# Sums of exponentials folded on VectorE instead of TensorE, and channel sums broadcast by way of DRAM

## The chip, the cores and the metric

The kernel runs on one core of a Trainium2 chip. The metric is the device time of one execution in microseconds (us), given as the median over runs. Lower is better. The core has TensorE (PE, with its weight loads listed apart as PEld), VectorE (DVE), ScalarE (ACT), GpSimd (POOL) and SyncE (SP, here only an issuer of DMAs). [...]

## What is computed

Two layers of a graph network on 16 graphs of 1024 nodes with 256 channels, all in float32. The parts that the change touches lie in the first layer:

```python
h = relu(layernorm(x))                                  # per graph: 1024 nodes x 256 channels
c = mean(h, axis=channels)                              # one number per node
A = abs(abs(sigmoid(c[None, :] - c[:, None]) - 0.5) - 0.5) * 2
Wg = adj * (A + A.T) * 0.5                              # 1024 x 1024
q = relu((h.T @ Wg) * para).T ; k, v = split(h @ kv_w)  # 4 heads of 64
attn = softmax(q @ k.T * scale)                         # over the 1024 keys
x = x + attn @ v
```

The second layer normalises again, multiplies by a normalised adjacency matrix and passes two linear maps with batch norms over all graphs and nodes. The kernel computes A from tanh(|difference| / 2), with the sums of h over the channels in place of the means.

## The kernel before

**Units and steps.** A graph's attention is cut into four units (L871): two channel chunks k (two heads each) by two halves f of 512 queries. A unit has four steps, and each step takes two blocks of 128 keys. `scores` (L851) multiplies a key block with 512 queries for both heads (keys on partitions, two heads by 512 queries in the free dimension) and ScalarE takes the exponential (L867). `Unit.add` (L880) adds the 8 tiles `p` of a unit up into `acc` on VectorE (L886, L889): what is left to sum for the softmax's denominators are the 128 partitions of `acc`. `Unit.values` (L891) multiplies p with the values, one step late, into `o`.

**The end of a unit.** When the last values are issued (step 0 of the next unit), `Unit.sums` (L911) multiplies `acc` with a 128x64 matrix of ones, once for each head; ScalarE copies the result to `row` (L919, a tile of the four-buffer tag "y"), and POOL's queue stores one row a head to DRAM and reads it back with the queries on partitions (L920, L925). Two steps later (three in graph 0), `Unit.finish` (L929) transposes the output `o` by head and query on TensorE into `ot`, and `add_output` (L940) takes the reciprocal (L943), scales (L944) and adds to x (L950). The sums' tile and `ot` share one PSUM buffer, tag "t".

**The order of the work** is written out by hand in `attention` (L957), which goes through 256 steps, 16 a graph, and emits for each: the step's scores; what is due at the top (finish, a background piece that asked for the top by yielding TOP); add_output; the two adds; the values of the step before; then background pieces. `background(b)` (L761) is a generator that yields the cost of each piece, mostly 1.71 for eight matmul instructions; the loop takes pieces until the graph's total times the elapsed share of its 16 steps is reached (L1002), and a TOP ends the step early. For a middle graph b the background is: keys of graph b+1 (4 pieces), its `queries` (14), its values (4), `aggregate` (L622) of graph b-1 (14 pieces, called the gather), then `prepare(b+2)` (L743), which weaves in `hidden(b-1)` (8). Between them go VectorE's and ScalarE's parts: `weigh` (L395), which makes the weights from the channel sums by Abs (L426), Tanh (L434) and a product with adj (L413), the second norm of graph b-1 (in queries) and the first norm of graph b+2 (in the gather, from piece 7). `take` (L488), the q sums (L496 to L522), `at` (L649 to L675, scaled at L646) and the batch statistics (L717) take TensorE's results off PSUM or prepare its operands. `soon` (L116) defers an action to the next piece.

**Channel sums.** `Norm` (L286) finds mean and variance on VectorE (L305, L307), the inverse square root on POOL (L82, L83), the shift on VectorE (L315 for the second norm, L318), and ScalarE's relu (L329) leaves the channel sums of a node block in `csum`, 128 partitions by 8 blocks. The Abs needs all 1024 sums in the free dimension of every partition: `columns_of` (L184) repeats each column over 128 elements (L189, tiles of tag "y"), `broadcast_row` (L195) transposes the eight blocks on TensorE (L200), and ScalarE copies them to `cbc` (L201).

**Graph 0's extra work.** `graph` (L231) combines blocks of the transposed adjacency on POOL and stores them to `aht_d` from tiles `two` and `one`, of tag "y" too; `degrees` (L212) sums the columns of adj.

```python
# the loop's body, in its order
made = scores(*unit.at, g)
...
    ended.finish()
if top:
    done += advance(bg)
...
    ended.add_output()
...
    unit.add(pr)
...
    last.values(g_last, prs)
    if g_last == NG - 1:
        last.sums()
...
while done < due and not top:
    cost = advance(bg)
```

## Time and profile before

| what | us |
|---|---|
| median of 3 runs (2646.86 to 2647.53) | 2647.13 |
| the profiled execution, whole | 2651.18 |
| its span, first to last instruction | 2649.3 |
| PE busy | 2571.1 |
| DVE busy | 1741.8 |
| ACT busy | 1335.5 |
| POOL busy | 561.2 |
| sums' matmuls (L917), busy | 65.8 |
| broadcasts' transposes (L200), busy | 18.1 |
| POOL issuing the sums' DMAs (L920, L925) | 37.5 + 98.2 |

Busy time is the union over an engine's instructions[...]. An instruction's idle time is what its engine waited just before it, with what ended the wait. A float32 matmul shows as two instructions, a transpose as one. The granted TensorE clock was 0.989 of full speed over the span.

### The profile page before, as it was taken

What the parts mean: (1) busy time and instruction counts of PE and PEld (TensorE: products, weight loads), DVE (VectorE), ACT (ScalarE), POOL (GpSimd) and SP (SyncE); (2) the same over time, 40 slices, a digit from 0 to 9 for tenths busy, and PEclk for the clock granted to TensorE, in tenths of its full rate; (3) what the DMA queues carried; (4) which work ended last, traced back from release to release, by engine and by line L of the source; (5) the groups of instructions that cost most, each with busy time, mean ns of one, the idle gap of its engine ahead of it and who ended that gap; (6) DMA issues with size and microseconds to landing.
All of it is one profiled execution on the core that took longest, in us unless ns stands there. A gap on an engine that the chain in (4) does not pass through costs nothing. (4 is left out here: it accounts for less than half of the span.)

```text
span 2649.3 us, 32166 instructions
## 1 busy us (share of the span) xinstructions
PE 2571.1 (97%) x11874; PEld 951.7 (36%) x11874; DVE 1741.8 (66%) x2766; ACT 1335.5 (50%) x1935; POOL 561.2 (21%) x648
## 2 busy tenths in 40 slices
PE   8979999999999999999999999999999999999994
PEld 3333333333333333333333333333333333334443
DVE  5648576766667675757666676757576675557675
ACT  5745454636364554546363645545463634335544
POOL 1451111021111111110211111111111112026653
PEclk9989999999999999999999999999999999999997
DMA  4453414242423323152525242332424232355559
GB/s 159 149 177 109 146 61 171 84 171 80 166 78 135 100 96 136 60 175 80 172 80 175 68 144 92 103 133 65 166 80 171 80 132 96 134 196 204 193 179 377
DMA packets 132870, 356.12 MB, mean 134 GB/s; under 512 B 19040, under 2 KB 35936, under 8 KB 126560
## 3 DMA queue, kind: packets, MB, share of 16 engines
q1 hardware_dynamic: 105952, 274.77, 29.7%
q0 software_dynamic: 26752, 79.20, 8.9%
q8 instruction: 96, 1.57, 0.2%
q14 instruction: 70, 0.57, 0.1%
HBM read 279.19 MB, written 74.72 MB: 134 GB/s over the span
## 5 line engine op out<-in xcount | busy, mean ns | idle before, releaser
L867 ACT ACTIVATE p<-sc 128x1024 f32<-128x1024 f32 x512 | 495.4, 1020 | 610.3 <-PE sc L859 609.8
L889 DVE TENSOR_TENSOR acc<-acc,p 128x1024 f32<-128x1024 f32 x384 | 470.9, 1226 | 135.5 <-ACT p L867 115.1
L859 PE MATMUL sc<-q,k 64*128 64x512 f32 x2048 | 510.2, 617 | 14.2 <-ACT p L867 14.2
L900 PE MATMUL o<-p,v 128*64 128x512 f32 x2048 | 497.6, 607 | 0.0
L159 PE MATMUL pg<-w,h_a 128*64 128x512 f32 x1600 | 358.1, 592 | 3.4 <-ACT k L600 1.7
L159 PE MATMUL pa<-aht,h_b 128*64 128x512 f32 x1536 | 343.7, 592 | 0.0
L859 PEld LDWEIGHTS sc<-q,k 64*128 64x128 f32 x2048 | 176.6, 186 | 335.0 <-issue 298.0
L920 POOL DMA_DIRECT2D sums_d<-row x64 | 37.5, 586 | 1031.8 <-ACT row L919 1031.8
L159 PE MATMUL py<-at,w 128*64 128x512 f32 x1024 | 230.4, 592 | 0.0
L900 PEld LDWEIGHTS o<-p,v 128*64 128x64 f32 x2048 | 124.6, 136 | 286.0 <-issue 284.5
L413 DVE SCALAR_TENSOR_TENSOR w<-w,adj 128x1024 f32<-128x1024 f32 x128 | 158.0, 1235 | 101.7 <-ACT w L434 97.8
L159 PEld LDWEIGHTS pg<-w,h_a 128*64 128x64 f32 x1600 | 115.5, 137 | 231.8 <-issue 213.1
L159 PEld LDWEIGHTS pa<-aht,h_b 128*64 128x64 f32 x1536 | 111.2, 137 | 212.6 <-issue 196.6
L713 ACT ACTIVATE y<-py,vec 128x512 f32<-128x512 f32 x128 | 87.6, 684 | 167.9 <-PE py L159 111.4
L426 ACT ACTIVATE w<-cbc,csum 128x512 f32<-128x512 f32 x256 | 170.0, 715 | 0.0
L886 DVE TENSOR_TENSOR acc<-p,p 128x1024 f32<-128x1024 f32 x64 | 78.9, 1233 | 109.3 <-ACT p L867 109.3
L714 POOL DMA_DIRECT2D y_d<-y x128 | 70.1, 547 | 316.1 <-ACT y L713 315.5
L434 ACT ACTIVATE w<-w 128x1024 f32<-128x1024 f32 x128 | 134.9, 1054 | 1.8
L488 DVE TENSOR_TENSOR w<-w,w 128x1024 f32<-128x1024 f32 x112 | 132.7, 1215 | 1.5
L925 POOL DMA_DIRECT2D inv<-sums_d x128 | 98.2, 771 | 138.7 <-DMA sums_d<-row 102.2
L159 PEld LDWEIGHTS py<-at,w 128*64 128x64 f32 x1024 | 74.3, 137 | 145.1 <-issue 128.2
L717 DVE BATCH_NORM_STATS2 stats<-y 128x6 f32<-128x512 f32 x128 | 85.4, 686 | 59.3 <-ACT y L713 57.4
(151 smaller groups left out, 2892.9 us busy)
## 6 DMA issues: line engine op xcount, KB each, us to landing
aht<-aht_d SPq DMA_DIRECT2D x224, 512.0 KB, 6.4
adj<-in_adj_dram SPq DMA_DIRECT2D x128, 512.0 KB, 4.4
y_d<-y POOLq DMA_DIRECT2D x128, 256.0 KB, 2.6
yin_f<-y_d SPq DMA_DIRECT2D x32, 1024.0 KB, 6.3
x<-in_x_dram SPq DMA_DIRECT2D x32, 512.0 KB, 5.0
para<-in_para_dram SPq DMA_DIRECT2D x64, 256.0 KB, 3.8
x_d<-x POOLq DMA_DIRECT2D x16, 1024.0 KB, 10.5
xo_f<-x_d SPq DMA_DIRECT2D x32, 512.0 KB, 8.7
```

The source lines that it names most:

```text
L159: nc.tensor.matmul(dst[r], left[:, r], right, start=start, stop=stop)
L413: nc.vector.scalar_tensor_tensor(w, w, 1.0, a, op0=ALU.add, op1=ALU.mult)
L426: nc.scalar.activation(w[:, t, :], cbc[:, q * FB : (q + 1) * FB], AF.Abs, bias=csum[:, th * TH + t : th * TH + t + 1], scale=-1.0,)
L434: nc.scalar.activation(made[i], made[i], AF.Tanh, scale=-0.5 / C)
L488: nc.vector.tensor_sub(block(i)[part], block(x)[part], block(y)[part])
L713: nc.scalar.activation(y, made, AF.Identity, bias=b1[:, j : j + 1])
L717: nc.vector.bn_stats(stats1[:, j, i, :], y)
L859: nc.tensor.matmul(sc[:, e, :], ks[b][k][r, m * P : (m + 1) * P], qs[b][k][r, f * FB : (f + 1) * FB], start=True, stop=True,)
L867: nc.scalar.activation(pr, sc, AF.Exp)
L889: nc.vector.tensor_add(self.acc, self.acc, pr)
L900: nc.tensor.matmul(self.o[r, :], vs[b][k][:, m, r], pr[:, e, :], start=(m == 0), stop=(m == NT - 1),)
L925: nc.gpsimd.dma_start(out=self.inv[:, :, e], in_=sums_d[u][e].rearrange("(j q) -> q j", q=P))
```

## The change

Two edits, each with its followers.

**Sums of exponentials.** `fold` turns one head's half of `acc` (128 x 512) in squares of 32 x 32 on VectorE into PSUM and reduces each square's rows: 128 x 16 partial sums `part`, in which partition 32a + r holds, for query c*32 + r, the sum over 32 of the partitions. The four groups of partitions are added by one matmul with `same`, a 128 x 128 matrix that is one where two indices are equal modulo 32; so each group of 32 partitions holds all sums, and four reciprocals, each on 32 partitions, take those that the partition needs. The first head is folded at the end of step 0, the second at the end of step 1, the matmul stands at the top of step 2 and the transposes of the output at the top of step 3, one step later than before (the last unit's folds both stand at the end of its step 0, the rest at the next top).

**Channel sums.** For graphs 1 to 15 `csum` is written to DRAM as it lies (32 contiguous bytes a partition) and read back by one DMA to all partitions, both on SP's queue. `cbc` then holds node t*128 + p at p*8 + t, and the Abs reads it with a step of 8 elements. Graph 0 keeps the way by TensorE. `prepare` loses a TOP piece of cost 1.0 for each graph, and so does the start of the background of graph 0. The norm and the sums' way by DRAM go into the gather from piece 3. `st6` and `mv` have one buffer instead of two.

```diff
@@ -69,13 +69,22 @@
     aht_d = dram.tile([7, NP // 2, P, TH, FB], F32, name="aht_d")
     y1_d = [dram.tile([P, HC, FB], F32, name=f"y1_d{i}") for i in range(B * NH)]
+    csum_d = [dram.tile([N], F32, name=f"csum_d{b}") for b in range(B)]
     dinv_d = dram.tile([N], F32, name="dinv_d")
-    sums_d = [dram.tile([2, FB], F32, name=f"sums_d{u}") for u in range(B * CC * NH)]
     UNITS = B * CC * NH
     seen = const.tile([P, 2, UNITS], F32, name="seen")
-    ones = const.tile([P, HD], F32, name="ones")
+    ones = const.tile([P, 1], F32, name="ones")
     nc.gpsimd.memset(ones, 1.0)
+
+    SQ = 32
+    NS = P // SQ
+    same = const.tile([P, NS, SQ], F32, name="same")
+    nc.vector.tensor_reduce(
+        same[:, 0, :], ident.rearrange("p (a r) -> p r a", r=SQ), AX.X, ALU.add
+    )
+    for i in range(1, NS):
+        nc.vector.tensor_copy(same[:, i, :], same[:, 0, :])
     def rsqrt(dst, src, add, tmp):
@@ -290,8 +299,8 @@
             def __init__(self, b, first):
                 tag = "a" if first else "b"
                 self.src = xs[b]
-                self.st6 = p2.tile([P, NT, 6], F32, tag="st6", name=f"st6_{tag}_{b}")
-                self.mv = p2.tile([P, NT, 2], F32, tag="mv", name=f"mv_{tag}_{b}")
+                self.st6 = p1.tile([P, NT, 6], F32, tag="st6", name=f"st6_{tag}_{b}")
+                self.mv = p1.tile([P, NT, 2], F32, tag="mv", name=f"mv_{tag}_{b}")
                 self.sm = p2.tile([P, 3, NT], F32, tag="lnsm", name=f"lnsm_{tag}_{b}")
                 self.csum = None
                 if first:
@@ -386,11 +395,23 @@
                     )
                 nc.vector.tensor_copy(ht[:, g * FB : (g + 1) * FB], pt)
-        def differences(b, cbs):
-
-            cbcs[b] = p1.tile([P, N], F32, tag="cbc", name=f"cbc_{b}")
-            broadcast_row(cbcs[b], cbs, f"c{b}")
+        def differences(b):
+
+
+            cbc = p1.tile([P, N], F32, tag="cbc", name=f"cbc_{b}")
+            cbcs[b] = (
+                cbc.rearrange("p (t q) -> p t q", t=NT)
+                if b == 0
+                else cbc.rearrange("p (q t) -> p t q", t=NT)
+            )
             weighers[b] = weigh(b)
+            if b == 0:
+                broadcast_row(cbc, columns_of(csums[b], f"c{b}"), f"c{b}")
+                return
+            nc.sync.dma_start(out=csum_d[b].rearrange("(p t) -> p t", p=P), in_=csums[b])
+            nc.sync.dma_start(
+                out=cbc, in_=csum_d[b].rearrange("(o n) -> o n", o=1).to_broadcast([P, N])
+            )
         def weigh(b):
@@ -424,8 +445,8 @@
                     made.append(w)
                     for t in range(TH):
                         nc.scalar.activation(
-                            w[:, t, :],
-                            cbc[:, q * FB : (q + 1) * FB],
+                            w[:, t, :].rearrange("p (t q) -> p t q", q=P),
+                            cbc[:, q * NT // NH : (q + 1) * NT // NH],
                             AF.Abs,
                             bias=csum[:, th * TH + t : th * TH + t + 1],
                             scale=-1.0,
@@ -740,14 +761,15 @@
                 yield from norm.half(half * NT // 2)
             nc.gpsimd.dma_start(out=x1_d[B - 1], in_=xs[B - 1])
+        def summed(b):
+            yield from Norm(b, True).all()
+            differences(b)
+            yield 0.0
+
         def prepare(b, products):
-            cbs = columns_of(csums[b], f"c{b}")
             yield from islice(products, 1)
-            yield TOP
-            differences(b, cbs)
-            yield 1.0
             w = weighers[b]
             for k in range(CC):
                 yield from weave(islice(products, 3), (0, islice(w, AHEAD // 2)))
@@ -761,10 +783,7 @@
         def background(b):
             if b == 0:
-                differences_1 = columns_of(csums[1], "c1")
-                yield TOP
-                differences(1, differences_1)
-                yield 1.0
+                differences(1)
                 for k in range(CC):
                     yield TOP
                     transposed(1, k)
@@ -776,6 +795,7 @@
                 yield from weave(
                     plain_queries(1), (0, norm), (0, w), (5, graph()), (7, degrees())
                 )
+                differences(2)
                 yield from islice(products, 2)
                 yield from prepare(2, products)
                 return
@@ -793,7 +813,7 @@
                 yield from weave(endings.pop(), (2, normed(b - 1)))
                 yield next(gather)
             if b + 2 < B:
-                yield from weave(gather, (7, Norm(b + 2, True).all()))
+                yield from weave(gather, (3, summed(b + 2)))
                 yield from prepare(b + 2, before)
             elif b + 2 == B:
@@ -908,22 +928,33 @@
                     self.os = p2.tile([P, FB], F32, tag="os", name=f"os_{self.name}")
                     nc.scalar.copy(self.os, self.o)
+            def fold(self, e):
+
+
+                if e == 0:
+                    self.part = p1.tile([P, 2, FB // SQ], F32, tag="part", name=f"part_{self.name}")
+                pt = ps_t.tile([P, FB], F32, tag="t", name=f"turned_{self.name}_{e}")
+                nc.vector.transpose(pt, self.acc[:, e, :])
+                nc.vector.tensor_reduce(
+                    self.part[:, e, :], pt.rearrange("p (c s) -> p c s", s=SQ), AX.X, ALU.add
+                )
+
             def sums(self):
-                u = self.index
-                pt = ps_t.tile([P, FB], F32, tag="t", name=f"sums_{self.name}")
-                for e in range(2):
-                    r = slice(e * HD, (e + 1) * HD)
-                    nc.tensor.matmul(pt[r, :], ones, self.acc[:, e, :], start=True, stop=True)
-                row = py.tile([P, FB], F32, tag="y", name=f"row_{self.name}")
-                nc.scalar.copy(row, pt)
-                nc.gpsimd.dma_start(
-                    out=sums_d[u], in_=row.rearrange("(e r) c -> e r c", r=HD)[:, 0, :]
+                pt = ps_t.tile([P, FB], F32, tag="t", name=f"sums_{self.name}")[:, : 2 * FB // SQ]
+                nc.tensor.matmul(
+                    pt,
+                    same.rearrange("p a r -> p (a r)"),
+                    self.part.rearrange("p e c -> p (e c)"),
+                    start=True,
+                    stop=True,
                 )
                 self.inv = p2.tile([P, FB // P, 2], F32, tag="inv", name=f"inv_{self.name}")
-                for e in range(2):
-                    nc.gpsimd.dma_start(
-                        out=self.inv[:, :, e], in_=sums_d[u][e].rearrange("(j q) -> q j", q=P)
+                for a in range(NS):
+                    r = slice(a * SQ, (a + 1) * SQ)
+                    nc.vector.reciprocal(
+                        self.inv[r].rearrange("p j e -> p e j"),
+                        pt[r].rearrange("p (e j a) -> p a e j", e=2, a=NS)[:, a],
                     )
             def finish(self):
@@ -940,7 +971,6 @@
             def add_output(self):
                 b, k, f = self.at
                 J, pt = FB // P, self.out
-                nc.vector.reciprocal(self.inv, self.inv)
                 nc.vector.tensor_mul(
                     self.os.rearrange("p (j e c) -> p j e c", j=J, e=2),
                     pt.rearrange("p (j e c) -> p j e c", j=J, e=2),
@@ -960,7 +990,7 @@
             steps = [(u, g) for u in units for g in range(NG)]
             per_graph = CC * NH * NG
             before = None
-            pending = []
+            at_top, at_end, adds = {}, {}, {}
             bg, done, total, top = iter(()), 0.0, 0.0, False
             for s in range(len(steps) + 2):
                 if s < len(steps):
@@ -978,15 +1008,13 @@
                     due = total * (s % per_graph + 1) / per_graph
                 else:
                     due += 5.1
-                ended = None
-                if pending and pending[0][1] <= s:
-                    ended = pending.pop(0)[0]
-                    ended.finish()
+                for action in at_top.pop(s, ()):
+                    action()
                 if top:
                     done += advance(bg)
                     top = False
-                if ended is not None:
-                    ended.add_output()
+                if s in adds:
+                    adds.pop(s)()
                 if s < len(steps):
                     for pr in made:
                         unit.add(pr)
@@ -994,11 +1022,13 @@
                     (last, g_last), prs = before
                     last.values(g_last, prs)
                     if g_last == NG - 1:
-                        last.sums()
-
-
-                        later_by = 3 if last.at[0] == 0 else 2
-                        pending.append((last, s + (later_by if last.index < UNITS - 2 else 1)))
+
+                        n = 0 if last.index == UNITS - 1 else 1
+                        for e in range(2):
+                            at_end.setdefault(s + n * e, []).append(lambda u=last, e=e: u.fold(e))
+                        at_top.setdefault(s + 1 + n, []).append(last.sums)
+                        at_top.setdefault(s + 1 + 2 * n, []).append(last.finish)
+                        adds[s + 1 + 2 * n] = last.add_output
                 while done < due and not top:
                     cost = advance(bg)
                     if cost is None:
@@ -1007,6 +1037,8 @@
                         top = True
                         break
                     done += cost
+                for action in at_end.pop(s, ()):
+                    action()
                 before = (steps[s], made) if s < len(steps) else None
             run(bg)
...
@@ -1051,7 +1083,7 @@
                 run(islice(products, 2))
                 for k in range(CC):
                     transposed(0, k, (1,))
-                differences(0, columns_of(csums[0], "c0"))
+                differences(0)
                 run(weave(products, (0, islice(weighers[0], AHEAD))))
                 load_x(1)
                 load_x(2)
...
```

More of the change, by code (lines that the diff above doesn't have):

```diff
@@ L1018, in layers @@
                     run(Norm(b, True).all())
-                    differences(b, columns_of(csums[b], f"c{b}"))
+                    differences(b)
                     for k in range(CC):
@@ L1339, in flag @@
     def flag(good):
-        nc.tensor.matmul(good[0:1, :], ext[:, 2:3], ones[:, 0:1], start=True, stop=True)
+        nc.tensor.matmul(good[0:1, :], ext[:, 2:3], ones, start=True, stop=True)
         nc.vector.tensor_scalar(bad, good[0:1, :], -1.0, float(P), op0=ALU.mult, op1=ALU.add)
```

## The prediction

> **What bounds the kernel now.** I read the page's first two parts, then the stretches, then the timeline of one graph. In part 1 the columns are busy time, share of the span and instructions; part 2 cuts the span into 40 slices.
>
> ```profile
> PE 2571.1 (97%) x11874; PEld 951.7 (36%) x11874; DVE 1741.8 (66%) x2766; ACT 1335.5 (50%) x1935; POOL 561.2 (21%) x648
> PE   8979999999999999999999999999999999999994
> ```
>
> TensorE is never free for long, so its queue sets the time. The stretches say where it isn't full. The first line is graph 6, the second graph 0 (stretch; length, PE, PEld, DVE, ACT and POOL busy; clock, DMA):
>
> ```profile
> 923.10:1068.30 145.20, 145.01 (x698) 51.91 (x696) 98.24 (x156) 74.11 (x109) 22.42 (x29) 1.00 0.34 117
> 61.80:196.90 135.10, 115.81 (x548) 42.81 (x546) 72.34 (x111) 78.62 (x116) 70.58 (x95) 0.92 0.48 160
> ```
>
> Graphs 1 to 13 start 145.2 us apart, each with PE covered throughout. Graph 0 has 19.3 us (135.1 - 115.8) without a matmul. The timeline there names the cause (start, length, instruction, idle time before it and its releaser):
>
> ```profile
> 174.97 0.59 ACT L919 COPY row<-sums 128x512 f32<-128x512 f32 x1 [19.63 <-DMA aht_d<-two]
> ...
> 176.54 3.40 PE L859 MATMUL sc<-q,k 64*128 64x512 f32 x8 [13.73 <-ACT p L867]
> ...
> 183.41 1.12 PE L200 MATMUL cbp_c<-ident,cb_c 128*128 128x128 f32 x4 [2.88 <-DVE v L617]
> ```
>
> `row` and the columns `cb` share the four "y" buffers with graph()'s `two` and `one`, whose stores hold them. ScalarE waits, the exponentials queue behind it, and TensorE stops.
>
> In the steady graphs the sums are plain PE work: a step where they run is 9.8 us long and its neighbour 8.9. In the lines below the sums' weights load at 926.79, and the next work's at 927.65: **0.86 us a unit**. The broadcast's eight transposes hold PE from 1043.39 to 1044.41: **1.02 us a graph**.
>
> ```profile
> 926.79 0.14 PEld L917 LDWEIGHTS sums<-acc,ones 128*64 128x64 f32 x2 [0.28 <-issue]
> 927.65 0.14 PEld L159 LDWEIGHTS pk<-ht,kvw_f 128*64 128x64 f32 x2 [0.29 <-issue]
> 1043.39 1.09 PE L200 MATMUL cbp_c<-ident,cb_c 128*128 128x128 f32 x8
> 1044.41 1.94 PE L900 MATMUL o<-p,v 128*64 128x512 f32 x8
> ```
>
> What decides is how far VectorE is behind at the top of a unit's third step (the next unit's step 2), since the new sums will stand there. Today the output transposes `ot` stand there on PE, and `inv` (L943) marks the same place on VectorE:
>
> ```profile
> 942.56 1.22 DVE L413 SCALAR_TENSOR_TENSOR w<-w,adj 128x1024 f32<-128x1024 f32 x1
> 943.69 0.20 DVE L943 RECIPROCAL inv<-inv 128x8 f32<-128x8 f32 x1
> 943.75 0.66 PE L935 MATMUL ot<-ident,os 128*128 128x128 f32 x4
> ...
> 980.93 0.66 PE L935 MATMUL ot<-ident,os 128*128 128x128 f32 x4
> 981.68 0.16 DVE L315 TENSOR_TENSOR lnsm_b<-lnsm_b,deg 128x4 f32<-128x4 f32 x1 [0.33 <-POOL lnsm_b L83]
> 981.96 0.20 DVE L943 RECIPROCAL inv<-inv 128x8 f32<-128x8 f32 x1
> ...
> 1018.25 0.18 DVE L943 RECIPROCAL inv<-inv 128x8 f32<-128x8 f32 x1
> 1018.57 0.65 PE L935 MATMUL ot<-ident,os 128*128 128x128 f32 x4
> 1052.76 1.28 DVE L717 BATCH_NORM_STATS2 stats<-y 128x6 f32<-128x512 f32 x2
> 1053.35 0.66 PE L935 MATMUL ot<-ident,os 128*128 128x128 f32 x4
> ```
>
> VectorE's earlier work ends 0.03 us after PE is ready, 1.1 after, 0.2 before, and 0.7 after (L717 ends at 1054.04). The same four numbers return in graphs 2 to 13. DVE's 66% is an average; at these four points it has no room, and today that costs nothing because nothing on PE waits for it there.
>
> [...]
>
> **The change, part by part.**
>
> 1. Sums leave PE at the unit's end: -0.86 x 64. Their ScalarE copy (0.59) and POOL's three DMA issues (37.5 + 98.2 us in all) go as well. Off the critical path in steady graphs, gain there nothing.
>
> 2. One 128x128 matmul of 32 columns comes at the top of step 2. `ot`'s four transposes add 0.59 us between scores and values, the broadcast's eight 1.02: some 0.11 each and 0.16 fixed. Two weight passes then give 0.16 + 2 x 0.11 = 0.37, less what loads during a wait; bounds 0.15 and 0.45, taken **0.3**. Four a graph: 1.2.
>
> 3. VectorE gets two folds a unit, each a transpose of 128x512 into PSUM and a reduce from it. The reduce is 0.69 like other 512-element PSUM reads. No transpose is in the trace; lower bound 512 elements at the rate of L889 ((1226 - 691) / 512 = 1.04 ns), 0.53; upper 1.2, the length of 1024 elements; taken 0.69. The reduce needs the transpose (dependent starts lie 0.72 apart: 938.25, 938.97), so **a fold is 1.42 us**, bounds 1.1 and 2.0. The first comes at the end of step 0, the second at the end of step 1, both behind the background's VectorE work.
>
> 4. The **new wait**: the sums matmul needs the second fold. Behind it on PE stand the TOP transposes, the values and all background products; they wait too. Stall = old lag + 1.42 + what the first fold pushed along:
>  - step 2: 0.03 + 1.42 = 1.45; with slower ScalarE (part 6) up to 2.65, since L413 waits for its tanh. Taken 1.75.
>  - step 6: 1.1 + 1.42, and the first fold falls in a solid stretch (968.5 to 980), of whose push 0.75 is left at the rsqrt on POOL that L315 waits for: 2.5 to 3.4, taken 3.2.
>  - step 10: -0.2 + 1.42 = 1.2; the norm now starts at the gather's third piece instead of its seventh, so shift(4,4), waiting for POOL (some 2 us), comes before the fold: up to 2.6, taken 1.75.
>  - step 14: the dropped TOP moves two products from step 13 into 12 and leaves one there; that is less time for the two adds (2.55), L413 and L717 before the fold: 1.4 to 2.3, taken 1.8.
>
>  Sum **8.5 us a graph**.
>
> 5. The broadcast's PE work goes for 15 graphs (-1.02 each), with two copies on VectorE and two on ScalarE, which had cover. In its place SP issues a write of csum and a 512 KB read. Nearest row: the read of `dinv_d`, 5.1 us to landing; the write some 2 (`sums_d` 1.7), at worst 10.6 like the write of `dinv_d`. Behind them on SP stand the adj loads. The first use is four background pieces and a step boundary later, about 12 to 15 us: covered at 7, and 1 to 3 us late a graph at 15.7. Taken 0, bound +3.
>
> 6. The Abs reads of cbc (L426, 0.715 us, 16 a graph) step by 32 bytes: 0 to +0.43 each (its 512 elements at half the rate). ScalarE's lag is covered by PE's queue except where part 4 counts it. In graph 0 ScalarE is full from 81 to 112: up to +3.
>
> 7. Four reciprocals on 32 partitions instead of one (0.19 each), in the shadow of values: 0, or +0.4 a unit if adds come late. add_output one step later: step 3 takes 1.7 us more of VectorE, which the idle of step 4 (1.29 + 1.55) absorbs: 0. `same` is built while the first x load is awaited: 0. One buffer for st6 and mv: norms lie a step or more apart, 0; else a POOL wait of 2 us.
>
> 8. Graph 0: no tile of the sums or broadcasts waits for `two`/`one`. Of the 19.3 us, the 0.5 to 0.9 us gaps near 64 to 90 stay; **-17.5**. POOL's chain ends sooner, and its first user comes in graph 1's step 4; nothing new is late.
>
> **The sum.** Steady graph: -3.44 - 1.02 + 1.2 + 8.5 = +5.24; thirteen: **+68**. Graph 0: -2.6 (three units) - 2.0 (two broadcasts) - 17.5 + 0.9 + 1.3 = **-20**. Graph 14 (lags -0.7, 0.4, -1.4, -0.5 at its four places): stalls 0.7 + 2.5 + 0 + 0.9, +1.2 - 3.4 = +2. Graph 15: 2.3 + 0.3 and 1.1 at the last unit, whose folds stand together, +1.2 - 3.4 = +1.5. Total **+51.5**. The profiled execution (span 2649.3, 2651.2 whole) would go to 2703; the runs' median lies 4 us lower: **2699**.
>
> **Rivals.** *A, the folds hide* and only the savings are left: 13 x (4.46 - 1.2) + 21 + 4 = 68 us, **2579**. For it: DVE is 34% idle. Against: the four lags. It decides at a fold plus push under some 0.9 us; at 1.1 us without push the sum is still about +11. *B, strided Abs and slow transposes*: stalls +1.35 and +2.3 a graph more, **2720 to 2745**. *C, the round trip by DRAM is late*: ScalarE stands before Abs, the exponentials behind it: up to +3 x 14, **2740**. *D, only graph 0 gains* (-20, +3.5 for graphs 14 and 15) and steady graphs break even: **2630**.
>
> **Chances.** My forecast (2655 to 2735) 62%; B and C 15%; A 11%; D and between 12%, of which about half lands within 0.2% or just over. Faster by over 0.2%: 0.17; within: 0.05; slower: 0.78. (0.2%, 5 us, is about what a measurement tells from no change.) The range leaves out most of A and the far end of B and C: 2628 to 2745.
>
> **What would show it.** PE idle before the new sums, released by a VectorE reduce, near 1.75, 3.2, 1.75, 1.8 us in each graph; 0.86 gone from step 0; no wait on `two` in graph 0; Abs at 0.71 or at 1.14; no ScalarE wait on cbc. If those idle times are under half a microsecond, or the fold is much under 1.4, the forecast is wrong and A holds.

## The result and the profile after

The changed kernel takes 2770.48 us (median of 4 runs, 2767.57 to 2774.67) against 2647.33 for the kernel before beside it: a ratio of 1.0467, 95% interval 1.0452 to 1.0483. The profiled execution has a span of 2767.0, 117.7 more than before. The direction was as predicted. The size was not: the forecast was +51.5.

First the page's first two parts. TensorE's busy time is the same as before to 0.3 us (2571.1), so the new time is time without TensorE work, or with work that is shown as busy but runs slowly. VectorE has 199 us more.

```profile
PE 2571.4 (93%) x11626; PEld 954.7 (35%) x11626; DVE 1941.0 (70%) x3188; ACT 1404.4 (51%) x1841; POOL 396.6 (14%) x456
...
PE   8899999999999999999999999999999999999995
```

Next the stretches, graph 6 and graph 0 (stretch; length, PE, PEld, DVE, ACT and POOL busy; clock, DMA), which answer to the two shown of before (145.20 and 135.10):

```profile
950.10:1103.70 153.60, 144.96 (x682) 51.94 (x680) 110.36 (x183) 78.81 (x103) 11.06 (x17) 0.98 0.34 113
62.00:180.80 118.80, 107.61 (x526) 39.52 (x524) 83.93 (x128) 86.26 (x109) 72.72 (x86) 1.00 0.61 202
```

A steady graph is 8.4 us longer. It has 8.6 us without TensorE work (153.60 - 144.96) where there was 0.2. It also has fewer matmul records (682 against 698) and yet the same busy time: the mean clock is 0.98, not 1.00. Graph 0 is 16.3 us shorter, no wait for `two` is left in it, and its clock is 1.00 where it was 0.92.

The third view is the timeline of graph 6 at the four places where the sums now stand: steps 2, 6, 10 and 14 (start, length, instruction, idle time before it and its releaser).

```profile
972.61 0.41 PE L945 MATMUL sums<-part,same 128*128 128x32 f32 x2 [2.60 <-DVE part L938]
...
1007.36 1.99 PE L879 MATMUL sc<-q,k 64*128 64x512 f32 x8
...
1010.68 0.16 DVE L324 TENSOR_TENSOR lnsm_b<-lnsm_b,deg 128x4 f32<-128x4 f32 x1 [0.33 <-POOL lnsm_b L92]
...
1010.96 0.72 DVE L937 STREAM_TRANSPOSE turned<-acc 128x512 f32<-128x512 f32 x1
1011.71 0.69 DVE L938 TENSOR_REDUCE part<-turned 128x16 f32<-128x512 f32 x1
...
1012.46 0.64 PE L945 MATMUL sums<-part,same 128*128 128x32 f32 x2 [3.11 <-DVE part L938]
...
1013.02 3.68 PE L920 MATMUL o<-p,v 128*64 128x512 f32 x8
...
1052.63 0.41 PE L945 MATMUL sums<-part,same 128*128 128x32 f32 x2 [0.35 <-DVE part L938]
...
1088.51 0.41 PE L945 MATMUL sums<-part,same 128*128 128x32 f32 x2 [2.58 <-DVE part L938]
```

At each, TensorE has finished the scores and waits for the second fold's reduce. The waits are 2.60, 3.11, 0.35 and 2.58 us: 8.64 together. Behind the wait of 3.11 comes the surprise. The eight matmul instructions of the values take 3.68 us; at the other steps, and in the kernel before, they take 1.94. The sums' own matmul takes 0.64 instead of 0.41.

The clock column shows why. These are five stretches of 3.41 us each around that wait, with the columns of the stretches above:

```profile
1005.11:1008.52 3.41, 3.41 (x18) 1.26 (x16) 3.38 (x14) 0.79 (x2) 0.00 (x0) 1.00 0.00 0
1008.52:1011.94 3.42, 0.83 (x4) 0.00 (x0) 3.02 (x8) 3.06 (x5) 2.50 (x3) 1.00 0.45 166
1011.94:1015.35 3.41, 2.90 (x8) 1.27 (x10) 2.51 (x7) 2.26 (x5) 0.00 (x0) 0.50 0.99 245
1015.35:1018.77 3.42, 3.42 (x16) 1.57 (x14) 1.22 (x1) 0.00 (x0) 0.00 (x0) 0.50 0.93 382
1018.77:1022.18 3.41, 3.41 (x36) 2.20 (x34) 2.11 (x5) 1.23 (x3) 0.00 (x0) 1.00 0.88 360
```

In the second stretch TensorE works for only 0.83 us. The next two have half the clock (0.50), 6.83 us in all, of which TensorE is busy for 6.31 (the first 0.52 belong to the wait). Half of that is lost: **3.15 us a graph**, in time that the page shows as busy.

Finally the durations of what the change added and altered: the groups of Abs and of the sums (busy, mean ns of one, idle before), then the tiles `turned` and `part`, and Abs in graph 6 alone (duration in ns as minimum, median, maximum).

```profile
L447 ACT ACTIVATE w<-cbc,csum 128x512 f32<-128x512 f32 x256 | 292.7, 1195 | 0.0
...
L945 PE MATMUL sums<-part,same 128*128 128x32 f32 x128 | 29.8, 318 | 132.7 <-DVE part L938 132.7
```

```profile
L937 DVE STREAM_TRANSPOSE turned<-acc x128: 693/719/726, 105.0 to 2438.5; 128x512 f32<-128x512 f32 x128
L938 DVE TENSOR_REDUCE part<-turned x128: 691/691/693, 105.8 to 2439.2; 128x16 f32<-128x512 f32 x128
...
L447 ACT ACTIVATE w<-cbc,csum x16: 1203/1230/1257, 956.3 to 1096.9; 128x512 f32<-128x512 f32 x16
```

A fold is 0.72 + 0.69 = 1.41 us. The waits for folds come to 132.7 us in the whole run. Abs with its step of 32 bytes takes 1.23 us instead of 0.715; the 1195 ns of the group is a mean that includes the 16 dense reads of graph 0, so where the expectations below say 1.195 and 0.48 us, it is 1.23 and 0.51. Abs waits for nothing (0.0), so `cbc` always comes in time by way of DRAM.

### The profile page after: what moved, and what is told of

Read it like the earlier page. It is cut to its first block, busy times and chain, and to the rows that moved or that the text cites. A ratio compares the mean times of both kernels' runs of the same rounds, so it can differ in the third digit from the quotient of the medians.

```text
span 2767.0 us, 31542 instructions
## 1 busy us (share of the span) xinstructions
PE 2571.4 (93%) x11626; PEld 954.7 (35%) x11626; DVE 1941.0 (70%) x3188; ACT 1404.4 (51%) x1841; POOL 396.6 (14%) x456
## 4 chain that ended last, share of the span: by engine, by line
PE 63%; DVE 20%; ACT 7%; issue 4%; DMA 3%; POOL 2%; SPq 0%; POOLq 0%; DVEq 0%; ACTq 0%
PE o L920 14%; PE pa L168 11%; PE sc L879 9%; PE pg L168 8%; PE m_f L1214 7%; PE py L168 6%; DVE acc L909 5%; PE pv L168 4%; ACT w L447 4%; DVE part L938 2%; DVE w L434 2%; DVE turned L937 2%; DMA out_dram<-xo_f 2%; PE ot L966 1%; DVE st_a L314 1%
## 5 line engine op out<-in xcount | busy, mean ns | idle before, releaser
L887 ACT ACTIVATE p<-sc 128x1024 f32<-128x1024 f32 x512 | 495.2, 1020 | 571.0 <-PE sc L879 570.6
L920 PE MATMUL o<-p,v 128*64 128x512 f32 x2048 | 523.5, 634 | 0.0
L168 PE MATMUL pa<-aht,h_b 128*64 128x512 f32 x1536 | 344.3, 593 | 0.7 <-ACT h_b L338 0.6
L447 ACT ACTIVATE w<-cbc,csum 128x512 f32<-128x512 f32 x256 | 292.7, 1195 | 0.0
L945 PE MATMUL sums<-part,same 128*128 128x32 f32 x128 | 29.8, 318 | 132.7 <-DVE part L938 132.7
L168 PE MATMUL pv<-kvw_f,ht 128*64 128x256 f32 x1024 | 130.9, 413 | 0.4 <-DVE v L638 0.4
L91 POOL TENSOR_SCALAR lnsm_b<-mv_b 128x4 f32<-128x4 f32 x32 | 12.2, 380 | 806.5 <-DVE mv_b L316 806.4
```

The lines of the kernel that those rows point to most:

```text
L168: nc.tensor.matmul(dst[r], left[:, r], right, start=start, stop=stop)
L447: nc.scalar.activation(w[:, t, :].rearrange("p (t q) -> p t q", q=P), cbc[:, q * NT // NH : (q + 1) * NT // NH], AF.Abs, bias=csum[:, th * ...
L887: nc.scalar.activation(pr, sc, AF.Exp)
L920: nc.tensor.matmul(self.o[r, :], vs[b][k][:, m, r], pr[:, e, :], start=(m == 0), stop=(m == NT - 1),)
```

## The experiments

All start from the changed kernel or from the kernel before, and all compute the whole output. "Pitch" is the length of a steady graph, from scores to scores (graphs 2 to 13; graph 1 is up to 1.6 us longer still).

| run | us, median | ratio to before (95%) | pitch |
|---|---|---|---|
| changed kernel | 2770.5 | 1.0467 (1.0452 to 1.0483) | 153.6 |
| late_sums | 2668.2 | 1.0080 (1.0063 to 1.0097) | 146.8 to 148.4 |
| one_unit | 2723.0 | 1.0288 (1.0268 to 1.0307) | 149.3 to 153.0 |
| dense_abs | 2706.1 | 1.0221 (1.0204 to 1.0238) | 150.0, two of 148.3 |
| longer_wait | 2793.9 | 1.0560 (1.0542 to 1.0577) | 154.3 and 156.3 in turn |
| placed | 2594.0 | 0.9793 (0.9779 to 0.9806) | 141.9 |
| early_dense | 2609.9 | 0.9854 (0.9839 to 0.9869) | 143.6 |
| csum_only | 2637.5 | 0.9953 (0.9940 to 0.9967) | 144.2 |
| fold_only | 2754.6 | 1.0394 (1.0378 to 1.0410) | 150.5 to 153.8 |
| placed_strided | 2599.6 | 0.9815 (0.9801 to 0.9828) | 142.0 |
| placed_tail | 2590.4 | 0.9781 (0.9768 to 0.9794) | 141.9 |

### late_sums: the sums one step later

```diff
-                        at_top.setdefault(s + 1 + n, []).append(last.sums)
-                        at_top.setdefault(s + 1 + 2 * n, []).append(last.finish)
-                        adds[s + 1 + 2 * n] = last.add_output
+                        at_top.setdefault(s + 1 + 2 * n, []).append(last.sums)
+                        at_top.setdefault(s + 1 + 3 * n, []).append(last.finish)
+                        adds[s + 1 + 3 * n] = last.add_output
```

> The changed kernel with the sums' matmul one step later (top of step 3 instead of step 2), the output's transposes and add_output at step 4; nothing else moved. My theory (TensorE waits at the sums for VectorE's second fold, 8.65 us a graph, and the longest of these waits halves the TensorE clock for some 4 us, 2.6 us a graph): the waits before the sums go to under 0.5 us each, the clock stays at 1.00 in step 6, a steady graph takes about 142.5 to 144 us instead of 153.6, and the time is 2600 to 2625, below the kernel before. Only the last unit's wait (4 us) stays. Rival 1 (VectorE has too much work in all, the wait only moves): the sums wait about as long at step 3, 2740 to 2770. Rival 2 (the strided reads of cbc or the way by DRAM cost the time): no change, about 2770.

It took 2668.2, so the expected 2600 to 2625 was wrong. The waits before the sums are gone in every unit but the last, as expected. Three places of the four now cost nothing. In step 6, however, TensorE waits as long as before, at another line:

```profile
972.87 0.72 DVE L937 STREAM_TRANSPOSE turned<-acc 128x512 f32<-128x512 f32 x1
...
974.23 2.54 DVE L909 TENSOR_TENSOR acc<-acc,p 128x1024 f32<-128x1024 f32 x2
...
976.69 0.75 DVE L638 COPY v<-pv 128x256 f32<-128x256 f32 x2
...
977.59 3.24 PE L168 MATMUL pv<-kvw_f,ht 128*64 128x256 f32 x16 [3.04 <-DVE v L638]
```

VectorE's queue is the fold, the two adds, then the copy that frees a PSUM buffer of `pv`. TensorE needs that buffer. What waits at step 6 is not tied to the sums: VectorE is late there, and the first matmul that needs anything from it waits. The first rival was right for one place in four, my theory for three.

### one_unit: both folds early for the unit that sums at step 6

```diff
-                            at_end.setdefault(s + n * e, []).append(lambda u=last, e=e: u.fold(e))
+                            at_end.setdefault(s + (0 if last.index % 4 == 0 else n * e), []).append(lambda u=last, e=e: u.fold(e))
```

> The changed kernel with both folds together at the end of step 0, but only for the one unit of each graph whose sums stand at step 6; the other three units as they were. My theory (that wait of 3.11 us and the half clock after it, 2.6 us, belong together): both go, 14 graphs by 5.7 us, about 2690; the clock of step 6 stays at 1.00. Rival (the clock falls at step 6 for another reason[...]): only the wait goes, 14 x 3.1 = 44 us, about 2727, and 12 values instructions in step 6 still show half the clock. Rival (the wait moves to another place): over 2745.

2723.0, not 2690. The wait of 3.11 is gone, but TensorE waits 1.79 us for `v` in step 6 (the first line after this paragraph, from the timeline of graph 6): the folds still stand in VectorE's full stretch. The half clock has not gone either, it has moved. In this run it follows the waits of 2.59 us at step 14 in ten of the graphs 1 to 13 (step 14 then takes 14.4 to 16.0 us instead of 12.8) and those at step 2 in four. The other two lines are stretches at step 14 of graph 6. The first rival has the right time, but its reason, a fall tied to step 6, is wrong. My idea that a wait must pass some 3 us for the clock to fall has fallen with it.

```profile
1005.42 1.95 PE L168 MATMUL pv<-kvw_f,ht 128*64 128x256 f32 x16 [1.79 <-DVE v L638]
...
1070.39:1073.80 3.41, 0.89 (x8) 0.89 (x9) 2.85 (x7) 2.82 (x3) 0.00 (x0) 1.00 0.76 231
1073.80:1077.21 3.41, 3.41 (x12) 1.23 (x12) 3.26 (x6) 0.00 (x0) 0.00 (x0) 0.50 0.00 0
```

### longer_wait: 0.72 us more at step 2

```diff
                 nc.vector.transpose(pt, self.acc[:, e, :])
+                if twice:
+                    nc.vector.transpose(pt, self.acc[:, e, :])
...
-lambda u=last, e=e: u.fold(e)
+lambda u=last, e=e: u.fold(e, e == 1 and u.index % 4 == 3)
```

> The changed kernel with one more transpose on VectorE (128x512, overwritten by the one that follows) ahead of the second fold of the one unit in each graph whose sums stand at step 2; it lengthens that wait by 0.72 us, from 2.6 to 3.3. My theory (a wait of somewhat over 3 us halves the TensorE clock for some 4 us, one of 2.6 doesn't): at step 2 the clock now falls to 0.5 as at step 6, 0.7 + 2.6 a graph, about 2770 + 45 = 2815. Rival (the clock falls at step 6 for a reason of its own, not for the wait's length): only the 0.7 a graph, about 2780, and the clock of step 2 stays at 1.00.

2793.9: neither. The wait at step 2 is 3.35 us in every graph, but the clock falls after it only in every other one. These stretches of 3.41 us stand around that wait in graph 3 (three lines) and graph 4 (two):

```profile
509.73:513.14 3.41, 2.43 (x12) 0.69 (x8) 3.31 (x4) 3.38 (x5) 0.00 (x0) 1.00 0.32 64
513.14:516.56 3.42, 1.04 (x6) 0.64 (x8) 2.82 (x7) 3.39 (x4) 0.00 (x0) 1.00 0.45 166
516.56:519.97 3.41, 3.41 (x10) 0.98 (x8) 3.14 (x5) 3.41 (x4) 0.00 (x0) 0.50 0.02 5
...
666.74:670.15 3.41, 1.73 (x8) 0.43 (x6) 3.31 (x4) 3.38 (x6) 0.00 (x0) 1.00 0.46 109
670.15:673.57 3.42, 1.73 (x10) 0.83 (x12) 2.68 (x8) 3.39 (x5) 0.00 (x0) 1.00 0.32 121
```

All these stretches lie on one grid, which the trace itself gives: every interval of half clock in it begins at a multiple of 3.413 us plus the same 1.14, and lasts 3.41 or 6.83 (but for the last, in which the execution ends). In graph 3 most of the wait lies in one cell of the grid (1.04 of 3.42 us busy), and the next cell has half the clock. In graph 4 the border cuts the wait in the middle (1.73 and 1.73), and the clock of the next cell stays at 1.00. The wait is as long in both graphs, so its length doesn't tell them apart; **how much of one cell it empties** does: 2.38 us of 3.42 in graph 3, 1.68 and 1.69 in graph 4.

The other traces agree: in each, the half-clock intervals start on one grid of 3.413 us. Here is a count of the cells at full clock in nine traces (the changed kernel and the eight runs from late_sums to fold_only), from 62 us to the last scores. With under 1.7 us without a TensorE record, 1 of 5738 is followed by half clock; with over 1.9 us, 106 of 110; between, 10 of 35. The borders of 1.7 and 1.9 were read from the traces themselves. The trace of the kernel before has no cell over 1.7 us between 190 and 2310 us, and no half clock there. So in these traces a cell that was a little over half empty was enough.

### dense_abs: Abs reads its row densely

```diff
-            nc.sync.dma_start(out=csum_d[b].rearrange("(p t) -> p t", p=P), in_=csums[b])
+            nc.sync.dma_start(out=csum_d[b].rearrange("(t p) -> p t", p=P), in_=csums[b])
...
-                            w[:, t, :].rearrange("p (t q) -> p t q", q=P),
-                            cbc[:, q * NT // NH : (q + 1) * NT // NH],
+                            w[:, t, :],
+                            cbc[:, q * FB : (q + 1) * FB],
```

> The changed kernel with the channel sums written to DRAM in the order of the nodes (4-byte pieces instead of 32-byte ones), so that cbc is in node order and ScalarE's Abs reads it densely (0.715 us again instead of 1.195). The folds are as in the change. My theory (the waits for the folds are the cost, the strided Abs only lengthens those at steps 2 and 14, where the tanh and so L434 come late): the waits at steps 2 and 14 fall from 2.6 to about 1.5, step 6 with its half clock stays, about 2740. Rival 1 (the strided Abs is what costs the time): 2660 or less. Rival 2 (Abs has cover everywhere): no change, 2765 to 2775. Rival 3 (1024 pieces of 4 bytes make the write too slow, ScalarE waits for cbc): above 2775.

2706.1, 64 us under the changed kernel, where 30 were expected. Abs is back at 715 ns. The waits at steps 2 and 14 fall to 1.38 and 1.58, as expected; that is 2.2 us of a graph. The wait of 3.10 at step 6 stays, but its half clock is one window (1.7 us) in place of two, and in graphs 3 and 11 none: the shorter pitch has shifted the waits on the grid. Here are graph 3, without a fall, and graph 4, with one, after the same wait of 3.10:

```profile
533.53:536.94 3.41, 1.93 (x10) 0.63 (x8) 3.05 (x11) 2.75 (x5) 2.09 (x3) 1.00 0.15 50
536.94:540.35 3.41, 1.79 (x10) 0.90 (x12) 2.77 (x9) 3.35 (x6) 0.40 (x1) 1.00 0.88 281
...
683.71:687.12 3.41, 0.31 (x4) 0.29 (x2) 2.68 (x6) 3.41 (x6) 1.91 (x2) 1.00 0.69 225
687.12:690.54 3.42, 3.42 (x10) 1.01 (x11) 3.08 (x6) 1.46 (x3) 0.00 (x0) 0.50 0.79 256
```

In the changed kernel the pitch of 153.6 us is 45 cells of 3.413, so from graph 2 on every graph met the grid in the same place and lost two windows (graph 1 lost three). That multiple need not be chance. In late_sums a graph that comes later against the grid leaves less of the halved window to work in, and loses less: from graph 2 to graph 6 TensorE's work in the halved window falls from 3.41 to 2.66 us, and the pitch from 147.18 to 146.82 (43 cells are 146.77). That the changed kernel is pulled in the same way is argued from this, not shown.

### csum_only and fold_only: each part by itself

csum_only is the kernel before with the change's `differences`, `summed`, `prepare`, `weigh` and `csum_d`; fold_only is the changed kernel with those as before.

> The kernel before with the channel sums' part of the change alone (by way of DRAM, read at a step of 32 bytes); the softmax's sums stay on TensorE. My theory (the strided Abs and the way by DRAM cost TensorE nothing unless folds stand behind them): 13 to 15 broadcasts of 1.02 us saved and 5 us in graph 0, no new wait, no half window in a steady graph, 2622 to 2638. Rival (the strided Abs, 16 x 0.48 = 7.7 us more of ScalarE a graph, delays TensorE by itself): waits at scores for p or at products for w, 2650 to 2700. The stall in graph 0 behind row should stay (row still shares its buffers), 10 us or more.

2637.5, at the upper edge. A steady graph is 1.0 us shorter (144.2 against 145.2), the broadcast's price. Abs takes 1.23 us here too, and no TensorE wait comes of it in a steady graph. Graph 0 keeps its stall, 2.7 us longer than before in all, since `row` still waits for the buffers of `two`:

```profile
142.74 0.58 ACT L930 COPY row<-sums 128x512 f32<-128x512 f32 x1 [13.44 <-DMA aht_d<-two]
...
183.62 0.58 ACT L930 COPY row<-sums 128x512 f32<-128x512 f32 x1 [17.61 <-DMA aht_d<-two]
```

> The kernel before with the softmax's sums folded on VectorE as in the change, and the channel sums broadcast on TensorE as before (Abs dense, the first norm again from the seventh piece). My theory: waits at steps 2, 6, 10, 14 of about 1.4, 3.1, 0.3 and 1.6 as in the dense kernel, one half window a graph: 150 to 152 us a graph, 2710 to 2735. Each window of 3.41 us with over 1.9 us without TensorE work is followed by one of half clock, none with under 1.7 us is. Rival (the waits come from the channel sums' part, by its strided Abs or its earlier norm): 2650 or less.

2754.6, 20 us over the expected end. The waits are 1.38, 3.10, 1.09 and 1.98; those at steps 10 and 14 are longer than expected, and the one at step 14 often costs a window of half clock as well. The stretches are graphs 6 (no half window) and 7 (two):

```profile
948.20:1098.70 150.50, 142.95 (x692) 51.76 (x690) 111.35 (x184) 71.68 (x105) 11.04 (x17) 1.00 0.32 112
1098.70:1252.50 153.80, 146.25 (x692) 52.90 (x690) 111.35 (x184) 71.69 (x105) 11.04 (x17) 0.98 0.33 110
```

PE's busy time differs by 3.3 us for the same 692 records: the half clock, seen as work. What the expectation says of the cells held but for four near its borders: three of about 1.9 to 2.0 us without a fall and one of 1.68 with one.

The parts don't add up: -12 and +105 us (each against the kernel before beside it) and +123 together. With the folds in the change's places the strided Abs costs 64 us (2770.5 - 2706.1). Without the folds TensorE shows no wait for it in a steady graph.

### placed, early_dense, placed_strided: the same folds elsewhere

In dense_abs's trace VectorE has 0.2 us free in step 3, 2.1 in 4 and 0.1 in 5 (in that of late_sums at most 0.2 in each), but over 4 in each of steps 0, 6, 8 and 12 of a graph, and 2.9 in step 7. The edit moves the folds there; placed and early_dense read `cbc` densely, placed_strided as in the change.

```diff
+                        ends, top_at, out_at = {
+                            0: ((2, 3), 4, 5),
+                            1: ((1, 1), 3, 4),
+                            2: ((0, 0), 2, 3),
+                            3: ((0, 0), 2, 3),
+                        }[last.index % 4]
...
-                            at_end.setdefault(s + n * e, []).append(lambda u=last, e=e: u.fold(e))
-                        at_top.setdefault(s + 1 + n, []).append(last.sums)
-                        at_top.setdefault(s + 1 + 2 * n, []).append(last.finish)
-                        adds[s + 1 + 2 * n] = last.add_output
+                            at_end.setdefault(s + ends[e], []).append(lambda u=last, e=e: u.fold(e))
+                        at_top.setdefault(s + top_at, []).append(last.sums)
+                        at_top.setdefault(s + out_at, []).append(last.finish)
+                        adds[s + out_at] = last.add_output
```

> The changed kernel with dense reads of cbc, as in the run before, and the folds put where VectorE is free in a steady graph's trace: both at the end of step 0 for the units that end at steps 12 and 16, both at the end of step 9 for the one that ends at step 8, and at the ends of steps 6 and 7 for the one that ends at step 4 (VectorE has only 0.1 us free in all of steps 3 to 5); sums and transposes follow one to two steps later. My theory (VectorE's lag at the points where TensorE first needs it, then a clock halved for whole windows of 3.41 us wherever a window holds over some 1.8 us without TensorE work): no wait over 0.5 us is left in a steady graph, no half window, the graph takes 145.2 - 4.5 + 1.7 = 142.4 us, and the time is 2590 to 2615, below the kernel before. Rival (the folds cost TensorE something by themselves, or VectorE is full whatever the place): waits of 1 us and more come up at other lines, 2650 or more.

2594.0, as expected. One wait of 0.24 us is left in a steady graph, and no half window; the clock is 1.00 and TensorE is busy for 141.76 of 142.00 us. VectorE does as much as in dense_abs (110.66 against 110.45 us):

```profile
880.50:1022.50 142.00, 141.76 (x684) 50.93 (x682) 110.66 (x182) 70.77 (x103) 12.93 (x17) 1.00 0.36 123
```

early_dense has both folds of every unit at the end of step 0 (`at_end.setdefault(s, [])`).

> The changed kernel with dense reads of cbc and both folds of every unit at the end of step 0, the sums at the top of step 2 as in the change. My theory: the three waits at steps 2, 10 and 14 go, but the folds of the unit that ends at step 4 stand in VectorE's full stretch, so TensorE waits some 2 us for v in step 6, in part of the graphs with a window of half clock (1.7 us): 144.5 to 146.5 us a graph, 2625 to 2655. Rival (it is the total of VectorE's work that counts, not its place): as the dense kernel with the change's places, about 2705.

2609.9, better than expected: the wait for `v` in step 6 is there in each graph (1.8 us, 23.6 in all), but no half window comes with it in a steady graph: no cell has over 1.9 us without TensorE work. placed moves the folds of two units a graph from here; the one wait that goes with them is worth 143.6 - 141.9 = 1.7 us a graph.

> The changed kernel with nothing altered but the places of the folds, the sums and the output's transposes, as in the run with the folds where VectorE is free; cbc is read at the step of 32 bytes, as in the change. My theory (the strided reads cost TensorE nothing by themselves; in the change they made the tanh late and so L434, behind which the second fold stood): no wait over 0.5 us in a steady graph, no half window there, 141.9 to 142.6 us a graph; 3 us more in graph 0 than with the dense reads; 2592 to 2605. Rival (16 x 0.48 us more of ScalarE a graph reach TensorE in another way): 2615 or more.

2599.6, as expected: 142.0 us a graph with Abs at 1.23 us. Graph 0 alone is longer than in placed, by 6.0 us where 3 were expected: TensorE waits there 4.2 us more, and one window of half clock follows. This is the change as it stands, with nothing altered but the order, and it is 171 us faster than the change.

### placed_tail: the last unit without folds

```diff
+                if self.index == UNITS - 1:
...
+                            nc.tensor.matmul(
+                                pt[:, 2 * j + e : 2 * j + e + 1],
+                                self.acc[:, e, j * P : (j + 1) * P],
+                                ones,
...
+                    nc.vector.reciprocal(self.inv.rearrange("p j e -> p (j e)"), pt[:, : 2 * J])
+                    return
```

> The run with the folds where VectorE is free (dense reads), and for the last unit alone no folds: its sums are taken by eight matmuls on TensorE (each 128 columns of acc as weights, one column of ones), which leaves them with the queries on partitions, and one reciprocal reads them. My theory (of the last unit's 10 us over the kernel before, the two folds are 4.0 - 1.2 us of wait, the wait of the transposes for inv 1.0 and the two half windows 3.2): the wait before the sums falls to 1.2 us, the eight matmuls take 1.5 to 3 us, the half windows after the last scores may go; 2586 to 2592, 2 to 8 us under that run. Rival (the tail is longer for another reason): 2593 to 2596, unchanged.

2590.4. The first fence below is from placed, the second from placed_tail.

```profile
2263.84 0.64 PE L941 MATMUL sums<-part,same 128*128 128x32 f32 x2 [4.00 <-DVE part L934]
...
2265.51 1.09 PE L962 MATMUL ot<-ident,os 128*128 128x128 f32 x4 [1.04 <-DVE inv L951]
```

```profile
2260.42 1.95 PE L945 MATMUL sums<-ones,acc 128*128 128x1 f32 x16
...
2262.67 1.01 PE L977 MATMUL ot<-ident,os 128*128 128x128 f32 x4 [0.30 <-DVE inv L953]
```

The waits of 4.00 and 1.04 are 0 and 0.30. The half clock that follows at once is one window, not two, but another comes 51 us later that placed doesn't have, so the clock gains nothing. From the last scores to the end it is 340.3 us instead of 344.3. (The two intervals of the ratios overlap, so it is the trace that shows this gain.)

The window of half clock at once after the sums goes against the count of the cells. The cell before it has only 0.30 us without a record:

```profile
2259.41:2262.82 3.41, 3.11 (x23) 2.16 (x20) 1.74 (x5) 1.76 (x4) 1.74 (x3) 1.00 0.38 144
2262.82:2266.24 3.42, 3.42 (x12) 1.24 (x13) 2.49 (x7) 0.00 (x0) 0.00 (x0) 0.50 0.16 61
```

1.95 us of that cell are the sixteen instructions of one column. The page shows them as busy, and the clock fell all the same. The cells of the count end at the last scores, before this one. From 62 us on, no other cell of any trace with under 1.5 us without a record was followed by half clock.

## Why the prediction was wrong in size

The mechanism of the wait was right: the sums wait for VectorE's second fold, at the four places named and in each steady graph, and what stands behind them on PE's queue waits too: at step 6 PE has no matmul from 1009.35 to 1012.46 us, and the values start at 1013.02, behind the sums, though the exponentials that they multiply (L887, step 5) ended at 1001.54. **The step that failed is "The sum"**. It charged each microsecond of wait as one microsecond and had no term for the clock. From the first scores to the end, half of TensorE's busy time at half clock is 59 us in the changed kernel and 8 in the kernel before. The difference of 51 is most of the 66 us by which the forecast missed (117.7 - 51.5). That a stall costs the clock was in view: the prediction's own line for graph 0 has a clock of 0.92.

By terms, measured against predicted:

- **Steady graphs**, +8.4 against +5.24. Without the half clock it is 8.4 - 3.15 = 5.25, so the rest of the sum holds. Thirteen graphs lose 43 us to the clock (3.15 each, 4.7 in graph 1), the largest part of the miss.
- **The four waits**, 8.64 against 8.5; the total is right by luck, since two pieces were too small by 0.8 each and one too large by 1.4. Step 6: 3.11 against 3.2. Steps 2 and 14: 2.60 and 2.58 against 1.75 and 1.8. Part 4 gave 1.45 for step 2 with Abs as before and up to 2.65 with slow Abs; dense_abs and the change measured 1.38 and 2.60. Both ends were right, and the value taken between them was wrong, because part 6's bound of +0.43 us an Abs is passed (+0.51). (That bound was an estimate; the trace of before has 0.43 us between the 1024 elements of L867, 1.02, and the 512 of L919, 0.59.) Step 10: 0.35 against 1.75. The earlier norm was thought to delay it; with the norm where it was before (fold_only), the wait is 1.09, so the trace speaks for the opposite. (fold_only also keeps the broadcast's copies on VectorE, so the norm's part isn't isolated.)
- **Savings less the new matmul**, 3.26 predicted. placed_strided has the same instructions as the change and a clock of 1.00; TensorE is busy for 141.76 us of its graph 6, against 145.01 before: 3.25.
- **Graph 14**, +7.7 against +2: waits of 6.2 instead of 4.1, and two half windows (2 x 1.7). **Graph 15 and what follows**, +16 against +1.5: a wait of 6.3 at its step 6, where 2.3 were expected, the last unit's 4.0 + 1.0 against 1.1, and five half windows after these, up to 2500 us, where the kernel before has none.
- **Graph 0**, -16.3 against -20, near it by luck: the stall behind `two` went as predicted, but three waits for folds came (3.8 us in all), and those for ScalarE's `p` and `k` grew from 2.2 to 7.4 us. Against these stand 4.6 us that the kernel before lost to half clock after the stall, which the prediction didn't count. In fold_only it is -13.9, in csum_only +2.7, so this gain is the sums' part.
- **Parts 5 and 7**, taken at nothing: they cost nothing in a steady graph. No ScalarE instruction waits for `cbc`, and the four reciprocals (0.2 us each) hold nobody but the last unit's `ot`.
- **A fold**, 1.41 us against 1.42.

Rival A, that folds hide, is false for the places in the change and nearly true for others: placed gave 2594 where A said 2579. Half of rival B was right, the strided Abs (1.23 us); the transposes weren't slow (0.72). C and D are refuted.

That the excess over placed_strided is the waits and the clock closes as a sum: 8.64 - 0.24 + 3.15 = 11.55 us, and the pitches differ by 153.6 - 142.0 = 11.6.

Open: what exactly TensorE's clock goes by. Cells of 1.7 to 2.0 us without a record went both ways, and one cell of placed_tail with 0.30, 1.95 us of it one-column instructions, was followed by half clock. Of halved cells some with 0.5 us of pause were followed by a second one (the changed kernel), and some with 0.7 were not (late_sums).

## What to carry to other kernels

When work moves from a full engine to one that is "only 70% busy", read that engine's free time step by step at the places where the full engine will need it; the same change cost 123 us with the folds in one place and saved 49 with them in another. A wait on TensorE had two prices in these runs, the wait and the clock after it: of the 3.41 us cells with over 1.9 us empty, 106 of 110 were followed by half clock, and each window of it cost up to 1.7 us, half its length (one or two in the steady graphs of these runs). And an instruction that gets slower on a covered engine is free only until something on the critical path is put behind it: the slower Abs cost TensorE no wait in csum_only's steady graphs, and 64 us in all where the folds stood in the change's places.

## What the runs showed of the hardware that was not expected

- The granted clock had two values in the steady graphs, 1.00 and 0.50, and switched only at the borders of a grid of 3.413 us. With the same wait of 2.59 us at step 14, that step of one_unit took 12.8 us in some graphs and 14.4 to 16.0, with half clock, in ten others; after the wait of 3.35 us in longer_wait the clock fell in every other graph.
- The pitch of the loop stood at a multiple of the grid: from graph 2 to 13 of the changed kernel it is 153.57 to 153.61 us (45 x 3.413 = 153.6), and in longer_wait two graphs together take 310.6 (91 x 3.413).
- ScalarE's Abs of 512 float32 takes 1.23 us when it reads them at a step of 32 bytes, and 0.715 when it reads them densely.
- VectorE turns 128 x 512 float32 in squares of 32 into PSUM in 0.72 us, at nearly the rate of the reduce from PSUM (0.69).
- Eight matmuls with 128 columns of `acc` as weights and one column of ones (16 instructions) took 1.95 us and left the sums on the queries' partitions without a transpose or a DMA. TensorE's clock was halved after them, though the cell had only 0.30 us without a record.
